# Layer-norm statistics by ScalarE's accumulated sums in a graph-network kernel

## The chip, the cores and the metric

The kernel runs on one core of a Trainium2 chip. The metric is the device time of one execution in microseconds (us). All times here come from repeated executions of the kernel before and from one execution that the hardware profiler recorded.

## The reference, cut to what matters

Four graph layers run one after the other on 4096 nodes with 256 features. Each adds its input to its result and normalises. The change touches the end of the second layer, where a norm with gain and offset is followed at once by the residual norm, and the top-p cut of the attention in that layer.

```python
def _layernorm(x, axis=-1, eps=1e-5):
    m = jnp.mean(x, axis=axis, keepdims=True)
    v = jnp.var(x, axis=axis, keepdims=True)
    return (x - m) / jnp.sqrt(v + eps)

def _top_p_attention(X, W1, W2, W3):
    q = X @ W1.T @ W2.T
    k = X @ W3.T
    probs = jax.nn.softmax(q @ k.T / TAU, axis=-1)
    idx = jnp.argsort(-probs, axis=-1)
    sp = jnp.take_along_axis(probs, idx, axis=-1)
    cs = jnp.cumsum(sp, axis=-1)
    keep_sorted = cs - sp < TOP_P
    ...
    return A / jnp.maximum(A.sum(-1, keepdims=True), 1e-12)

# _L1_gnn_ref: R is the normalised adjacency plus identity
for n in range(STEPS):          # STEPS = 2
    A = _top_p_attention(Xa, W1, W2, W3)
    Xf = R @ Xf
    Xa = A @ Xa
    Z = Z + Xf @ U1[n].T + Xa @ U2[n].T
h = X + Z
mu = h.mean(-1, keepdims=True)
var = jnp.mean((h - mu) ** 2, axis=-1, keepdims=True)
return (h - mu) / jnp.sqrt(var + LN_EPS) * ln_g + ln_b

# reference
x = _layernorm(x + _L0_gnn_ref(x, adj, L0_gnn_W), axis=-1)
x = _layernorm(x + _L1_gnn_ref(x, adj, ...), axis=-1)
x = _layernorm(x + _L2_gnn_ref(x, adj, L2_gnn_H_v), axis=-1)
x = _layernorm(x + _L3_gnn_ref(x, adj, adj, L3_gnn_weight, L3_gnn_bias), axis=-1)
```

## The kernel before

The nodes are cut into 32 blocks of 128 rows. The first three blocks of the adjacency are treated as dense, and the others through lists of their non-zero columns, whose rows GpSimd (POOL) gathers with indirect DMAs. The first 450 us compute layer 0, the next 550 us the first attention step. Then comes the loop that the change touches: the second attention step, one row block after the other, in `for I in range(NT + 1)` with NT = 32. A round I of that loop works on several blocks at once:

- block I+3: TensorE computes its logits (L630), and ScalarE (ACT) their exponentials (L701, and L704 with half the scale) in the first slots of the round;
- block I+2 and I+3: ACT evaluates sums of a threshold guess over the whole row (`sums`: L740 with Relu, L746 with Sign), and POOL moves the threshold by a chain of some twelve tiny operations (`secant`, L754 and L757);
- block I+1: VectorE (DVE) keeps the values over the threshold and sorts them (`keep_few`: L821, the MAX8 of L827, sorts in L804 and L806, the boundary value u), and then cuts the row at u with its ties counted (`cut`: L857 to L869, then L872 and the MATCH_REPLACE8 of L873);
- block I: TensorE turns the cut row in eight groups (L224), ACT copies each to SBUF (`eT`, L226), and TensorE multiplies (`psa`, L235); this is `weighted_sum`, which hands out a slot of other work in each group. The product with R for the same block runs in those slots (`r_ahead`, L1057 and L1062, gathers at L371);
- block I-1: `out_1`, the end of the layer: the two norms and the store. It is a generator in pieces. L1009 takes the product out of PSUM, `norm_scale` gives the statistics, L1013 applies the first norm on ACT, POOL applies gain, offset and residual (L1014 to L1016), `norm_scale` runs again, L1021 applies the second norm on ACT, L1023 on DVE computes the score of the next layer, and x2 is stored.

The whole loop stands under a schedule written by hand: for TensorE, ACT, DVE and POOL, instructions run in the order of the calls. SyncE's DMA queue is not part of it. Each `steps(gen)` runs a generator to its next `yield`; that is how the pieces are placed. `end` is the generator of `out_1`. In a round it is moved on at these places:

```python
            steps(few)
            steps(end)
            steps(few)
            ...
                    if g == 0:      # first slot of weighted_sum
                        run(second_sum)
                        run(first)
                        evals = at[I + 2]["sums"] if I + 2 < NT else none
                        steps(few)
                        steps(end)
                        steps(few)
```

The first of these, with the kernel before, is the first `norm_scale`, and the second is L1013 with POOL's three operations. `run(second_sum)` ends with L746, and `run(first)` is POOL's secant. The other places are in the printed function below, after `run(slot)`: `steps(end)`, then `steps(guessed)`, `run(guessed)`, `steps(end)`, and after `steps(cuts)` a `run(end)`, which runs what is left.

`ud` (L845) is u times -1.2 * 2^-24, computed on POOL, and the instruction at L865 makes from it the four thresholds of the cut: u itself, or a value just under u where ties are kept. `down8` holds 0 to -7 for the drop of surplus ties (L872). If the guarded test at the end (`failed`) finds a row that the fast path can't hold, a branch over all columns runs as well.

Of the kernel before, what the change touches and what calls it, by code (L numbers as in the profile page):

```python
# [11 lines left out]
F32 = mybir.dt.float32  # L12
BF16 = mybir.dt.bfloat16
I32 = mybir.dt.int32
AF = mybir.ActivationFunctionType
OP = mybir.AluOpType
AX = mybir.AxisListType

P = 128
N = 4096  # L20
D = 256
DA = 64
NT = N // P
EPS = 1e-5
# [28 lines left out]
FETCH = 3  # L53
LEAD, SPREAD = (5, 12), 0.75
NM = 4
GUESS = (1.2, -0.129)
SLOPE, AIM, NEAR, MOVE, FEW = 0.07, 16, 32, 1.5, 70
EXP_BITS = float(2 ** 23 / np.log(2))
# [16 lines left out]
def gnn_kernel(ctx: ExitStack, tc: tile.TileContext, x, pair, panels, W0, W1, W2T, W3T, U1T, U2T,  # L75
               ln_g, ln_b, Hv, W3L, b3, hubs, out):
    nc = tc.nc
    PSUM = bass.MemoryType.PSUM
    const = ctx.enter_context(tc.tile_pool(name="const", bufs=1))
# [44 lines left out]
    def one(name, dtype=F32, bufs=2):  # L124
        return small.tile([P, 1], dtype, name=name, tag=name, bufs=bufs)
# [40 lines left out]
        return t  # L166

    iota8 = iota([8], "iota8", [[1, 8]])
    down8 = const.tile([P, 8], F32, name="down8")
    nc.vector.tensor_scalar_mul(down8, iota8, -1.0)  # L170
    row = const.tile([P, 1], I32, name="row")
    nc.gpsimd.iota(row, [[1, 1]], base=0, channel_multiplier=1)

# [635 lines left out]
    def keep_few(a):  # L809


        I, e, s = a["I"], a["e"], a["s"]
        f = facts[1]["f"][:, I:I + 1]
        cand = pools["w2"].tile([P, NS, 8], F32, name="cand", bufs=1)
        ex = pools["w2"].tile([P, TOP], F32, name="ex", bufs=1)
        h = a["h"]
        low = small.tile([P, 2], F32, name="low")
        for c in range(2):
            w = tmp_tile([P, N // 2])
            ec = e[:, c * (N // 2):(c + 1) * (N // 2)]  # L820
            nc.vector.scalar_tensor_tensor(w, ec, h, ec, op0=OP.is_lt, op1=OP.mult, accum_out=low[:, c:c + 1])  # L821
            nc.gpsimd.tensor_scalar(f, low[:, c:c + 1], -1.0, f if c else s, op0=OP.mult, op1=OP.add)
            if c:
                nc.gpsimd.tensor_copy(ex[:, 0:1], f)
            yield
            for g in range(NS // 2):
                nc.vector.max(cand[:, c * (NS // 2) + g, :], w[:, g * SEG:(g + 1) * SEG])  # L827
            yield
        tgt = a["tgt"]
        nc.vector.tensor_reduce(facts[1]["h"][:, I:I + 1], cand[:, :, 7], AX.X, OP.max)  # L830
        top = pools["w2"].tile([P, TOP], F32, name="top", bufs=1)
        rest = pools["w2"].tile([P, NS * 8], F32, name="rest", bufs=1)
        sort_top(top, cand.rearrange("p a b -> p (a b)"), rest, TOP)
        nc.vector.tensor_tensor_scan(ex[:, 1:], ones.to_broadcast([P, TOP - 1]), top[:, :TOP - 1], f, op0=OP.mult, op1=OP.add)
        nc.gpsimd.tensor_copy(facts[1]["x"][:, I:I + 1], ex[:, TOP - 1:])
        kv = pools["w2"].tile([P, TOP], F32, name="kv", bufs=1)
        k = one("ks")
        nc.vector.scalar_tensor_tensor(kv, ex, tgt, top, op0=OP.is_lt, op1=OP.mult, accum_out=k)
        u, r = facts[1]["u"][:, I:I + 1], facts[1]["r"][:, I:I + 1]
        nc.vector.scalar_tensor_tensor(top, ex, tgt, top, op0=OP.is_ge, op1=OP.mult)  # L840
        nc.vector.tensor_reduce(u, top, AX.X, OP.max)
        nc.vector.tensor_scalar(kv, kv, u, 0.0, op0=OP.is_equal, op1=OP.add, accum_out=r)
        nc.vector.tensor_add(k, k, f)
        ud = a["ud"] = one("ud")
        nc.gpsimd.tensor_scalar(ud, u, -1.2 * 2.0 ** -24, None, op0=OP.mult)  # L845
        a["kr"], a["rk"] = one("kr", bufs=3), one("rk", bufs=3)
        nc.gpsimd.tensor_scalar(a["kr"], k, rinv[:, I:I + 1], None, op0=OP.mult)
        nc.vector.reciprocal(a["rk"], k)
        a["cand"], a["rest"] = cand, rest

    def cut(a):


        n, I, e, cand, rest = 1, a["I"], a["e"], a["cand"], a["rest"]
        u, r = facts[n]["u"][:, I:I + 1], facts[n]["r"][:, I:I + 1]
        ties = small.tile([P, NM], F32, name="ties")
        nc.vector.tensor_scalar(rest, cand.rearrange("p a b -> p (a b)"), u, None, op0=OP.is_equal)  # L857
        nc.vector.tensor_reduce(ties, rest.rearrange("p (a b) -> p a b", a=NM), AX.X, OP.add)
        left = small.tile([P, NM], F32, name="left")
        nc.vector.tensor_tensor_scan(left, ones.to_broadcast([P, NM]), ties, r, op0=OP.mult, op1=OP.subtract)  # L860
        nc.vector.tensor_add(ties, ties, left)
        nc.vector.tensor_scalar(ties, ties, 0.0, None, op0=OP.is_gt)
        d = facts[n]["d"][:, I:I + 1]
        nc.vector.scalar_tensor_tensor(left, left, 0.0, ties, op0=OP.min, op1=OP.mult, accum_out=d)
        nc.vector.tensor_scalar(ties, ties, a["ud"], u, op0=OP.mult, op1=OP.add)  # L865
        m = N // NM
        for g in range(NM):
            eg = e[:, g * m:(g + 1) * m]
            nc.vector.scalar_tensor_tensor(eg, eg, ties[:, g:g + 1], eg, op0=OP.is_gt, op1=OP.mult)  # L869
        yield  # L870
        drop = small.tile([P, 8], F32, name="drop")
        nc.vector.tensor_scalar(drop, down8, d, u, op0=OP.is_gt, op1=OP.mult)  # L872
        nc.vector.match_replace(e[:, ::-1], drop, e[:, ::-1], 0.0)  # L873

    def failed():
# [4 lines left out]
        for n in range(2):  # L880
            s, f, u, h, x, r = (facts[n][k] for k in "sfuhxr")
            nc.vector.tensor_tensor(c, h, u, op=OP.is_lt if n else OP.is_le)
            nc.vector.tensor_mul(ok, ok, c)
            if n:
                nc.vector.tensor_scalar(c, s, TOP_P, None, op0=OP.mult)
                nc.vector.tensor_tensor(x, x, c, op=OP.is_ge)
                nc.vector.tensor_mul(ok, ok, x)
                nc.vector.tensor_tensor(f, f, c, op=OP.is_lt)
                nc.vector.tensor_mul(ok, ok, f)
                nc.vector.scalar_tensor_tensor(ok, facts[n]["d"], -8.0, ok, op0=OP.is_ge, op1=OP.mult)  # L890
            else:
                nc.vector.scalar_tensor_tensor(ok, u, 0.0, ok, op0=OP.is_gt, op1=OP.mult)
                nc.vector.scalar_tensor_tensor(c, r, 1 - 2.0 ** -14, u, op0=OP.mult, op1=OP.is_gt)
                nc.vector.tensor_mul(ok, ok, c)
                nc.vector.scalar_tensor_tensor(ok, listed[:, :, 1], float(NB * P), ok, op0=OP.is_le, op1=OP.mult)
            nc.vector.scalar_tensor_tensor(ok, s, 1e-25, ok, op0=OP.is_gt, op1=OP.mult)
            nc.vector.scalar_tensor_tensor(ok, s, 1e35, ok, op0=OP.is_lt, op1=OP.mult)
# [81 lines left out]

    scores = const.tile([P, NT], F32, name="scores")  # L980

    def to_shift(m, rs):
        t = one("shift")
        nc.gpsimd.tensor_scalar(t, m, rs, -1.0, op0=OP.mult, op1=OP.mult)
        return t

    def scaled_rest(a, psr):

        xf = work.tile([P, D], F32, name="xf2", tag="nb")
        nc.scalar.activation(xf, psr[:, :D], AF.Copy, scale=a["kr"])  # L990
        return xf

    def norm_scale(st_of):
        st = small.tile([P, nc.vector.BN_STATS_DIM], F32, name="st")
        nc.vector.bn_stats(st, st_of)
        mv = small.tile([P, nc.vector.BN_AGGR_DIM], F32, name="mv")
        nc.vector.bn_aggr(mv, st)
        ve, rs = one("ve"), one("rs")
        nc.gpsimd.tensor_scalar(ve, mv[:, 1:2], EPS, None, op0=OP.add)
        nc.gpsimd.tensor_tensor(rs, ve, neg_half, OP.pow)  # L1000
        return rs, to_shift(mv[:, 0:1], rs)

    def out_1(a, psa):

        I = a["I"]
        x0 = pools["late"].tile([P, D], F32, name="x0")
        nc.sync.dma_start(x0, tab[rows(I), :D])
        h = work.tile([P, D], F32, name="y")
        nc.scalar.activation(h, psa[:, :D], AF.Copy, scale=a["rk"])  # L1009
        yield  # L1010
        rs, shift = norm_scale(h)
        yield
        nc.scalar.activation(h, h, AF.Identity, scale=rs, bias=shift)  # L1013
        nc.gpsimd.tensor_add(x0, x0, bb)  # L1014
        nc.gpsimd.tensor_mul(h, h, gb)
        nc.gpsimd.tensor_add(h, h, x0)  # L1016
        yield
        rs, shift = norm_scale(h)
        yield
        x2 = pools["late"].tile([P, D + 2], F32, name="x2", tag="o")  # L1020
        nc.scalar.activation(x2[:, :D], h, AF.Identity, scale=rs, bias=shift)  # L1021
        yield
        nc.vector.scalar_tensor_tensor(h, x2[:, :D], 1.0, hvb, op0=OP.mult, op1=OP.mult, accum_out=x2[:, D + 1:])  # L1023
        nc.gpsimd.memset(x2[:, D:D + 1], 1.0)
        nc.gpsimd.tensor_copy(scores[:, I:I + 1], x2[:, D + 1:])
        nc.sync.dma_start(x2d[rows(I), :], x2)
# [792 lines left out]
```

## Time and profile before

| | us |
|---|---|
| median of 11 runs | 2536.13 |
| lowest and highest run | 2533.56 and 2542.25 |
| the profiled execution, its own time | 2528.12 |
| its span, first to last instruction | 2526.3 |

Busy time in that span: PE (TensorE's matmuls) 2117.9, its weight loads (PEld) 1520.1, DVE 2087.4, POOL 1612.5, ACT 1477.2.

The span begins with the first instruction and ends with the last. Times in the views are us from the start of the span. A line such as L1013 is a line of the kernel before. The letter x with a number counts instructions; a bracket names the idle time ahead of an instruction and the engine and line that ended it. The page's rows of digits cut the span into 40 equal slices of 63 us, and each digit is the busy share in tenths. An instruction that gives a sum is followed by a readout (ACTIVATION_READ_ACCUMULATOR or DVE_READ_ACCUMULATOR) on the same engine.

The instructions that the change removes or touches, from the trace (median of one, in ns): bn_stats at L995 421 (x64), bn_aggr at L997 182 (x64), `ve` at L999 236, the power at L1000 568, `shift` at L984 264, `ud` at L845 240 (x32), L1009 475 (x32), L1013 608 (x32), L1021 619 (x32), POOL's L1015 727 (x32).

### The profile page before, as it was taken

Reading aid. Unit: us, or ns where it says so; the run is one execution under the profiler, and the core shown is the slowest. Engines: PE = TensorE matmul, PEld = TensorE weight load, DVE = VectorE, ACT = ScalarE, POOL = GpSimd, SP = SyncE. Lnnn points to the kernel's source line nnn. Section 1 sums busy time; section 2 is a strip of 40 time slices with the busy share of each in tenths; the row PEclk is TensorE's granted clock in tenths of the full one; section 3 lists DMA queues with packets and bytes.
Section 4 is the critical chain, followed back from the end, with each engine's and each line's share of the span. In section 5 each row is a group of like instructions: output and inputs, shape, how many; then the busy total and the mean of one; then the engine's idle time right before and its main releaser. Section 6 shows DMA issues by size and latency. Waiting matters only on the chain.

```text
span 2526.3 us, 37676 instructions
## 1 busy us (share of the span) xinstructions
PE 2117.9 (84%) x10692; PEld 1520.1 (60%) x10692; DVE 2087.4 (83%) x6433; ACT 1477.2 (58%) x2455; POOL 1612.5 (64%) x2648
## 2 busy tenths in 40 slices
PE   7888988799988887698888788888888877788995
PEld 5666666356555555576665566656656666556774
DVE  4788876799999983665899899999999996688588
ACT  0111111488888885565888889999999972434100
POOL 3343433366666665434888888888888883766375
PEclk8999999799999999899899999999999998899998
DMA  9887875456555556455111111111111123888795
GB/s 304 290 273 243 300 228 167 119 169 169 146 145 138 152 140 180 153 159 158 58 44 51 49 46 43 45 45 45 45 44 45 44 59 92 273 277 272 219 300 161
DMA packets 252842, 371.90 MB, mean 147 GB/s; under 512 B 40176, under 2 KB 161536, under 8 KB 252624
## 3 DMA queue, kind: packets, MB, share of 16 engines
q1 hardware_dynamic: 162528, 212.27, 26.3%
q0 software_dynamic: 41936, 120.07, 17.5%
q10 hardware_dynamic: 48160, 37.05, 4.4%
q8 instruction: 88, 1.44, 0.2%
q14 instruction: 130, 1.06, 0.1%
HBM read 314.23 MB, written 55.02 MB: 146 GB/s over the span
## 4 chain that ended last, share of the span: by engine, by line
DVE 30%; PE 14%; ACT 5%; POOL 4%; issue 4%; DMA 3%; DVEq 0%; SPq 0%; ACTq 0%; POOLq 0%
DVE cand L827 5%; DVE e L873 4%; PE acc L1620 4%; PE psa L235 4%; DVE tmp L821 4%; DVE e L869 3%; PE acc L1057 2%; DVE top L804 2%; DVE rest L806 2%; ACT junk L740 2%; POOL xg L371 1%; PE pt L224 1%; DVE vt L267 1%; PE lg L630 1%; DMA t3d<-t 1%
## 5 line engine op out<-in xcount | busy, mean ns | idle before, releaser
L235 PE MATMUL psa<-v,eT 128*128 128x256 f32 x2048 | 506.1, 394 | 74.3 <-ACT eT L226 74.0
L235 PEld LDWEIGHTS psa<-v,eT 128*128 128x128 f32 x2048 | 395.5, 197 | 150.3 <-ACT eT L226 96.1
L516 PE MATMUL acc<-xw,panel 128*128 128x257 f32 x1024 | 253.4, 395 | 16.9 <-DMA xw<-in_x 16.9
L740 ACT ACTIVATE junk<-e,h 128x4096 bf16<-128x4096 f32 x64 | 237.4, 3710 | 38.9 <-POOL h L720 28.3
L224 PE MATMUL pt<-ident,e 128*128 128x128 f32 x1024 | 158.9, 286 | 107.7 <-DVE e L873 64.1
L516 PEld LDWEIGHTS acc<-xw,panel 128*128 128x128 f32 x1024 | 194.1, 196 | 61.6 <-issue 30.3
L746 ACT ACTIVATE junk<-e,h 128x4096 bf16<-128x4096 f32 x62 | 230.8, 3722 | 0.1
L224 PEld LDWEIGHTS pt<-ident,e 128*128 128x128 f32 x1024 | 131.1, 148 | 151.9 <-issue 108.8
L827 DVE MAX8 cand<-tmp 128x8 f32<-128x128 f32 x1024 | 203.8, 276 | 1.1
L226 ACT COPY eT<-pt 128x512 f32<-128x512 f32 x256 | 144.9, 588 | 95.2 <-PE pt L224 94.5
L371 POOL DMA_INDIRECT pc<-in_pair,idx_a x130 | 127.9, 984 | 96.1 <-PE lists_ps L331 37.8
L1118 DVE MAX8 cand<-e 128x8 f32<-128x256 f32 x512 | 176.3, 411 | 3.7 <-ACT e L1110 3.7
L1148 ACT ACTIVATE marks<-e,mid 128x1024 bf16<-128x1024 f32 x128 | 140.2, 1143 | 50.6 <-DVE mid L1144 46.4
L371 POOL DMA_INDIRECT xg<-x2d,idx_x x130 | 131.6, 1012 | 54.8 <-issue 23.8
L371 POOL DMA_INDIRECT xg<-ttab,idx_x x130 | 128.6, 989 | 53.6 <-issue 24.1
L371 POOL DMA_INDIRECT xg<-qtab,idx_x x130 | 123.5, 950 | 59.2 <-issue 28.9
L869 DVE SCALAR_TENSOR_TENSOR e<-e,ties 128x1024 f32<-128x1024 f32 x128 | 156.0, 1281 | 2.9
L701 ACT ACTIVATE e<-lg 128x1024 f32<-128x1024 f32 x120 | 123.2, 1027 | 51.3 <-PE lg L630 51.3
L821 DVE SCALAR_TENSOR_TENSOR tmp<-e,h 128x2048 f32<-128x2048 f32 x64 | 150.7, 2355 | 2.3
L1107 PE MATMUL lg<-kT,qi 64*128 64x512 f32 x512 | 145.3, 643 | 3.3 <-DVE want L356 2.8
L630 PE MATMUL lg<-kT,qi 64*128 64x512 f32 x480 | 136.0, 643 | 14.3 <-ACT junk L704 14.0
L371 POOL DMA_INDIRECT xg<-y3d,idx_x x111 | 106.5, 960 | 64.6 <-PE acc L1620 42.1
(345 smaller groups left out, 5361.2 us busy)
## 6 DMA issues: line engine op xcount, KB each, us to landing
panel<-in_panels SPq DMA_DIRECT2D x200, 256.0 KB
e<-in_panels SPq DMA_DIRECT2D x64, 512.0 KB
pc<-pk SPq DMA_DIRECT2D x78, 256.0 KB
xg<-ttab SPq DMA_DIRECT2D x96, 128.0 KB
kT<-in_hubs SPq DMA_DIRECT2D x24, 512.0 KB
pc<-in_panels SPq DMA_DIRECT2D x32, 256.0 KB
tab<-xi ACTq DMA_DIRECT2D x33, 160.0 KB
pc<-pk SPq DMA_DIRECT2D x15, 320.0 KB
```

The lines of the kernel that those rows point to most:

```text
L224: nc.tensor.transpose(pt[:, k, :], e[:, (g * 4 + k) * P:][:, :P], ident)
L235: nc.tensor.matmul(ps[:, :D], eT[g][:, k, :], rhs[j][:, :D], start=(j == 0), stop=stop and j == NT - 1)
L371: nc.gpsimd.indirect_dma_start(out=o, out_offset=None, in_=src, in_offset=bass.IndirectOffsetOnAxis(ap=idx[:, c], axis=0))
L516: nc.tensor.matmul(ps[:, :D + 1], a[:, k, :], XW[j][:, :D + 1], start=(j == 0), stop=(j == NT - 1))
L630: nc.tensor.matmul(ps[:, h, :], qi[r, :], kT[r, (n * NC + c) * LC:][:, :LC], start=True, stop=True)
L740: nc.scalar.activation(junk_tile(), e, AF.Relu, bias=h, scale=-1.0, accum_out=part)
L746: nc.scalar.activation(junk_tile(), e, AF.Sign, bias=h, scale=-1.0, accum_out=below)
L821: nc.vector.scalar_tensor_tensor(w, ec, h, ec, op0=OP.is_lt, op1=OP.mult, accum_out=low[:, c:c + 1])
L827: nc.vector.max(cand[:, c * (NS // 2) + g, :], w[:, g * SEG:(g + 1) * SEG])
L869: nc.vector.scalar_tensor_tensor(eg, eg, ties[:, g:g + 1], eg, op0=OP.is_gt, op1=OP.mult)
L1107: nc.tensor.matmul(a["lg", c][:, k, :], a["qi"][r, :], kT[r, c * LC:(c + 1) * LC], start=True, stop=True)
L1118: nc.vector.max(a["cand"][:, b, :], a["e"][:, b * SEG0:(b + 1) * SEG0])
```

## The change

Both layer norms in `out_1` get their statistics from ACT instead of from DVE's bn_stats and bn_aggr. ACT's copy out of PSUM (L1009) also gives the sum of each row; POOL turns it into the negative mean; ACT squares the centred row and gives the sum of squares; POOL makes the scale and the shift. For the second norm, whose input POOL has just computed, ACT first copies the row for its sum. The output of the copy and of the squares goes to a bf16 tile, `aside`, which nobody reads. A `yield` between POOL's three operations and the second `norm_scale` is gone.

`ud` and POOL's operation for it are gone. The marks of kept ties carry the factor -2^-24 (`STEP`) and the thresholds are (marks + 1) times u; the count of surplus ties is scaled by the same factor, so `down8` becomes `up8` with the opposite test, and the guarded test compares with -8 STEP.

```diff
+STEP = -2.0 ** -24
-    down8 = const.tile([P, 8], F32, name="down8")
-    nc.vector.tensor_scalar_mul(down8, iota8, -1.0)
+    up8 = const.tile([P, 8], F32, name="up8")
+    nc.vector.tensor_scalar_mul(up8, iota8, -STEP)
 ...
-        ud = a["ud"] = one("ud")
-        nc.gpsimd.tensor_scalar(ud, u, -1.2 * 2.0 ** -24, None, op0=OP.mult)
 ...
-        nc.vector.tensor_scalar(ties, ties, 0.0, None, op0=OP.is_gt)
+        nc.vector.tensor_scalar(ties, ties, 0.0, STEP, op0=OP.is_gt, op1=OP.mult)
 ...
-        nc.vector.tensor_scalar(ties, ties, a["ud"], u, op0=OP.mult, op1=OP.add)
+        nc.vector.tensor_scalar(ties, ties, 1.0, u, op0=OP.add, op1=OP.mult)
 ...
-        nc.vector.tensor_scalar(drop, down8, d, u, op0=OP.is_gt, op1=OP.mult)
+        nc.vector.tensor_scalar(drop, up8, d, u, op0=OP.is_lt, op1=OP.mult)
 ...
-    def norm_scale(st_of):
-        st = small.tile([P, nc.vector.BN_STATS_DIM], F32, name="st")
-        nc.vector.bn_stats(st, st_of)
-        mv = small.tile([P, nc.vector.BN_AGGR_DIM], F32, name="mv")
-        nc.vector.bn_aggr(mv, st)
-        ve, rs = one("ve"), one("rs")
-        nc.gpsimd.tensor_scalar(ve, mv[:, 1:2], EPS, None, op0=OP.add)
-        nc.gpsimd.tensor_tensor(rs, ve, neg_half, OP.pow)
-        return rs, to_shift(mv[:, 0:1], rs)
+    def aside():
+        return small.tile([P, D], BF16, name="aside", bufs=1)
+
+    def norm_scale(total, y):
+
+        m, v, rs = one("m_y"), one("v_y"), one("rs")
+        nc.gpsimd.tensor_scalar(m, total, -1.0 / D, None, op0=OP.mult)
+        nc.scalar.activation(aside(), y, AF.Square, bias=m, accum_out=v)
+        nc.gpsimd.tensor_scalar(v, v, 1.0 / D, EPS, op0=OP.mult, op1=OP.add)
+        nc.gpsimd.tensor_tensor(rs, v, neg_half, OP.pow)
+        shift = one("shift")
+        nc.gpsimd.tensor_scalar(shift, m, rs, None, op0=OP.mult)
+        return rs, shift
 
     def out_1(a, psa):
 ...
-        nc.scalar.activation(h, psa[:, :D], AF.Copy, scale=a["rk"])
-        yield
-        rs, shift = norm_scale(h)
+        total = one("total")
+        nc.scalar.activation(h, psa[:, :D], AF.Copy, scale=a["rk"], accum_out=total)
+        yield
+        rs, shift = norm_scale(total, h)
         yield
         nc.scalar.activation(h, h, AF.Identity, scale=rs, bias=shift)
         nc.gpsimd.tensor_add(x0, x0, bb)
         nc.gpsimd.tensor_mul(h, h, gb)
         nc.gpsimd.tensor_add(h, h, x0)
-        yield
-        rs, shift = norm_scale(h)
+        total = one("total")
+        nc.scalar.activation(aside(), h, AF.Copy, accum_out=total)
+        rs, shift = norm_scale(total, h)
         yield
         x2 = pools["late"].tile([P, D + 2], F32, name="x2", tag="o")
         nc.scalar.activation(x2[:, :D], h, AF.Identity, scale=rs, bias=shift)
```

More of the change, by code (lines that the diff above doesn't have):

```diff
@@ L889, in failed @@
                 nc.vector.tensor_mul(ok, ok, f)
-                nc.vector.scalar_tensor_tensor(ok, facts[n]["d"], -8.0, ok, op0=OP.is_ge, op1=OP.mult)
+                nc.vector.scalar_tensor_tensor(ok, facts[n]["d"], -8.0 * STEP, ok, op0=OP.is_le, op1=OP.mult)
             else:
@@ L980, in gnn_kernel @@
     scores = const.tile([P, NT], F32, name="scores")
[L982 to L985, printed above, removed]
     def scaled_rest(a, psr):
```

## The prediction

> **What bounds the kernel now.** I read first the page's head and its 40 slices, to find the stage that the change touches:
>
> ```profile
> span 2526.3 us, 37676 instructions
> DVE  4788876799999983665899899999999996688588
> ACT  0111111488888885565888889999999972434100
> ```
>
> The two norms run in slices 18 to 34, where VectorE (DVE) and ScalarE (ACT) both show 8 and 9. Windows of 100 us inside it (columns: stretch, its length, then busy time of PE, PE's weight loads, DVE, ACT, POOL, the granted clock, the DMA share, GB/s):
>
> ```profile
> 1500.00:1600.00 100.00, 82.02 (x391) 60.54 (x389) 95.55 (x261) 91.24 (x113) 84.74 (x166) 0.98 0.14 43
> 1600.00:1700.00 100.00, 82.92 (x400) 61.06 (x400) 95.90 (x265) 91.72 (x112) 85.93 (x170) 1.00 0.14 42
> ```
>
> DVE is the bound (the missing 4% are hand-overs), but ACT and POOL are close behind. Next the order of one round of the loop over row blocks, engine by engine, in the timeline (start, length, instruction). ACT:
>
> ```profile
> 1566.60 1.06 ACT L226 COPY eT<-pt 128x512 f32<-128x512 f32 x2
> 1567.54 0.62 ACT L1021 ACTIVATE x<-y,shift,rs 128x256 f32<-128x256 f32 x1
> ...
> 1576.98 3.71 ACT L746 ACTIVATE junk<-e,h 128x4096 bf16<-128x4096 f32 x1
> ...
> 1580.68 0.59 ACT L1013 ACTIVATE y<-y,shift,rs 128x256 f32<-128x256 f32 x1
> 1581.17 0.57 ACT L226 COPY eT<-pt 128x512 f32<-128x512 f32 x1
> ```
>
> POOL:
>
> ```profile
> 1580.87 2.23 POOL L754 TENSOR_SCALAR below<-below 128x1 f32<-128x1 f32 x1 [0.84 <-ACT junk L746]
> ...
> 1587.04 0.30 POOL L754 TENSOR_SCALAR h<-h,b 128x1 int32<-128x1 int32 x1
> ...
> 1587.80 0.73 POOL L1014 TENSOR_TENSOR x<-x,bb 128x256 f32<-128x256 f32 x1
> 1588.48 0.73 POOL L1015 TENSOR_TENSOR y<-y,gb 128x256 f32<-128x256 f32 x1
> 1589.29 0.73 POOL L1016 TENSOR_TENSOR y<-y,x 128x256 f32<-128x256 f32 x1
> ```
>
> DVE:
>
> ```profile
> 1564.43 4.87 DVE L869 SCALAR_TENSOR_TENSOR e<-e,ties 128x1024 f32<-128x1024 f32 x4
> 1569.22 0.42 DVE L1023 SCALAR_TENSOR_TENSOR y<-x,hvb 128x256 f32<-128x256 f32 x1
> ...
> 1569.96 4.41 DVE L873 MATCH_REPLACE8 e<-drop,e 128x4096 f32<-128x4096 f32 x1
> ...
> 1574.67 2.35 DVE L821 SCALAR_TENSOR_TENSOR tmp<-e,h 128x2048 f32<-128x2048 f32 x1
> ```
>
> What to see: each engine runs exactly in the order in which the code calls it. After L1013 ACT goes on at once with an eT copy, which TensorE needs, while POOL finishes the sum h (L1016) only at 1590.02. First L995 of a round: 1561.46, next round 1593.62, so this round takes 32.16. Rounds are counted by the loop variable I. From the end of L746's readout in round 3 (1209.64) to that in round 29 (2059.84) there are 26 rounds in 850.2 us, 32.7 each.
>
> **Work moved.** Off DVE: bn_stats and bn_aggr, twice a round. Start to start they occupy 0.54 (1561.46 to 1562.00) and 0.56 (1576.94 to 1577.50): 1.10 per round, so DVE's own work is 32.16 - 1.10 = 31.06. Onto ACT: a readout at L1009 (0.19 long, the next instruction starts 0.09 after it), two Squares (nearest row L1013, 0.61, plus readout: at most 0.75) and a Copy with its sum (nearest row L936, 0.51, plus readout: 0.6). That is about 1.9 per round in occupancy. ACT's waits in this round (0.52, 0.65, 0.27, 0.75, 0.66, 0.48, all on TensorE) sum to 3.33, so ACT works 28.8 and would work 30.7. On POOL each norm goes from three tiny operations to four (+0.25 each, priced by L999's 0.24), less `ud` (0.24). By work alone nothing passes DVE's 31.06. [...]
>
> **Ties and up8.** The new constants leave the number of DVE instructions as it is; STEP takes `ud`'s place. DVE waited 28.4 us in all for `ud`, 16.2 of it in round 2, nothing in the steady rounds. What that frees in rounds 2 to 10 goes into the new waits below.
>
> **Three new waits**, from the code's order. (1) The Copy that sums h stands right behind L1013 on ACT and needs L1016. Behind it on ACT wait the second Square, the eT copies of this block, the exponentials of a later one, L740 and L746, and on them TensorE. (2) The first Square needs POOL's m, which POOL queues behind L822, which needs DVE's L821; behind the Square are eT copies and L746. (3) One yield is gone, so each later piece of `out_1` runs one call of `steps(end)` sooner. L1021 keeps its place on ACT (nothing lies between). L1023, which needs it, moves on DVE from behind L869 to ahead of L857, so the whole cut waits for ACT.
>
> **One round walked through**, t = 0 at the end of L746's readout.
> POOL's secant needs that readout: hand-over 0.09, `below` 0.19 (its smallest duration), the following operations to the end of h 4.14 (1583.20 to 1587.34), from L822 to the end of L1016 2.69. L1016 ends at 7.2. In the trace `below` took 2.23, ending at 1583.10 just after DVE's L821 (1583.04); if that recurs, 9.2. [...] In the new order DVE is in its MAX8 by then, and beside MAX8 the rows from 1583.20 on ran at their usual lengths, so I take 7.2 and keep 9.2 for the range.
> ACT: Copy 0.6, POOL's m with hand-overs 0.45, Square 0.75: t = 9.0. Then three slots, each an eT copy and two exponentials, 2.47 (1581.17 to 1583.64): 7.4. TensorE has run ahead, so its waits there vanish. From L740 to the end of L1021 9.8 (1558.36 to 1568.16): t = 26.2.
> DVE: hand-over 0.1, L1023 0.42, the cut from L857 to the end of L869 7.18 (1562.04 to 1569.22), from the drop to the end of L821's readout 7.46 (1569.56 to 1577.02): t = 41.4. (POOL's second secant starts at 24.7, takes 4.7, and its seven last operations end by about 36 even if L869 holds them: not late. ACT is through L740, two exponentials and L1009 at about 33: not late.)
> POOL: L822 and m with hand-overs 0.8. ACT: Square 0.7, two eT copies 0.95, L746 with readout 3.8: the next round's zero is at **47.6**.
> Cross-check on DVE: work 31.06; its last sort ends 16.2 after L821 (t = 10.0) and it then stands until 26.3, so 31.06 + 16.2 = 47.3. DVE goes from bound to waiter, and the ring ACT, DVE, POOL, ACT sets the time.
>
> **Sum.** 26 rounds: 26 x 47.6 - 850.2 = +387. Rounds 1 and 2 have TensorE's dense blocks (32 terms spread over 8 slots), which hide most of the stall. In round 1 L1023 already waited for L1021 until 1149.56; the cut and the rest behind it put the next L746 off by about 13. In round 2 TensorE reaches the product that needs the delayed eT copy at 1169.27, ACT gives it at about 1170.5; there +4. Round 29 lacks the exponentials: +9; rounds 30 and 31 have no secant: +4; the tail after the last L1009 gains a Copy and two round trips: +2. Total 387 + 17 + 15 = +419. The profiled execution took 2528.1 (span 2526.3 plus 1.8); with the change 2947. The median of the runs is 2536.1, 8 more, so **2955**.
>
> **Rivals.** *Faster:* the waits are covered, DVE stays the bound, each round falls to 31.06, and some of the 28.4 for `ud` comes back: 30 x 1.1 to that plus 28, 2475 to 2503. For it: DVE at 96%. Against it: ACT has 3.3 of slack, and the work takes 1.9 of that, so any stall over 1.4 decides; the order says 6.7 (from L1013's end at 0.5 to 7.2). *Only ACT's waits count:* if L1023 does not hold the cut, DVE has finished it by 24 and after L1023 needs 7.46: 34.2, then 6.2: a round of 40.4. That is 26 x 7.7 + 20 = +220: 2756. Against it: nothing in the code puts L1023 behind L857. *A longer ring:* the only ACT_TABLE_LOAD in the trace takes 1.28 us; if Square needed its own table, four switches a round are 5.1, all on the ring, +133: 3088. Against it: Copy, Sign, Relu, Identity and Exp share one load now. Or SP's queue puts x2d's store, which waits for POOL's L1024 at about 36, ahead of the next qi load; then the exponentials end near 41 and the ring is hardly longer. *It does not do what it says:* if the new thresholds did not cut where the old ones do, the kernel's guarded branch over all columns would run too, beyond any range here; but 1 - 2^-24 times u still rounds to the next number below u.
>
> **How the numbers follow.** Forecast ring 0.79; only ACT's waits 0.08; longer ring 0.09; faster 0.03; the branch 0.01. A ring of 44, if hand-overs and the four nearest-row prices are all too high and TensorE's head start does more, gives 2536 + 26 x 11.3 + 31 = 2861; a held secant, 49.6, gives 3007. I reach a little to both neighbours: 2830 to 3050. About 5 us (0.2%) is what a measurement can tell from no change. Faster 0.03, same 0.01, slower 0.96.
>
> **What would show it.** Right: L1023 idles some 16 us a round on ACT's L1021; the Copy idles about 6.7 on POOL's h; the first Square idles some 9 on m; DVE near 65% busy in the loop, POOL's gathers unchanged, stages before 1110 and after 2150 the same length. Wrong: eT copies that start right after L1013, a cut ahead of L1023, a second table load, or a round under 44 or over 50.

## The result, and the profile after

The changed kernel takes 3064.1 us (median of 8 runs, 3058.8 to 3071.1), the kernel before 2537.0 (31 runs): 1.207 times as long, 95% interval 1.206 to 1.2087. The direction was forecast, the mechanism too, but 3064 lies 14 us over the stated range and 109 over the forecast. The profiled execution took 3064.2 us, its span 3062.4.

The page's head and slices, as shown of before:

```profile
span 3062.4 us, 37734 instructions
DVE  5788867999995553746464646465656565568778
ACT  0111116888876655565656565665656565244300
PEclk8999998999999888777777777777777777889998
```

In the loop neither DVE nor ACT shows an 8 any more: no engine is the bound by its work, each one waits in turn. The granted clock, 0.97 over the loop before (1205 to 2050), is at 7 tenths (0.77 from 1200 to 2550). A window of the steady part, to set beside those of before:

```profile
1900.00:2000.00 100.00, 63.28 (x252) 45.20 (x252) 57.34 (x161) 60.50 (x83) 45.04 (x107) 0.77 0.10 28
```

DVE fell from 96 to 57, ACT from 92 to 60. One round in the timeline. The new lines are one off the old ones: L747 was L746, L1012 was L1013, L1015 was L1016, L868 was L869, L872 was L873, L822 was L821, and so are L227, L631, L702, L705, L716, L741 and L755; L994 is the Square, L1017 the Copy for the sum, L1021 and L1023 are as before. ACT:

```profile
1906.88 0.51 ACT L994 ACTIVATE aside<-y,m_y 128x256 bf16<-128x256 f32 x1 [8.37 <-POOL m_y L993]
...
1912.03 0.59 ACT L1012 ACTIVATE y<-y,shift,rs 128x256 f32<-128x256 f32 x1
1919.34 0.42 ACT L1017 ACTIVATE aside<-y 128x256 bf16<-128x256 f32 x1 [6.72 <-POOL y L1015]
...
1925.46 1.02 ACT L702 ACTIVATE e<-lg 128x1024 f32<-128x1024 f32 x1 [1.70 <-PE lg L631]
...
1929.76 0.58 ACT L227 COPY eT<-pt 128x512 f32<-128x512 f32 x1 [2.18 <-PE pt L225]
1930.83 1.02 ACT L702 ACTIVATE e<-lg 128x1024 f32<-128x1024 f32 x1 [0.48 <-PE lg L631]
```

POOL and DVE of the same round:

```profile
1912.21 0.19 POOL L755 TENSOR_SCALAR below<-below 128x1 f32<-128x1 f32 x1 [3.40 <-ACT junk L747]
...
1918.59 0.72 POOL L1015 TENSOR_TENSOR y<-y,x 128x256 f32<-128x256 f32 x1
```

```profile
1909.56 2.35 DVE L822 SCALAR_TENSOR_TENSOR tmp<-e,h 128x2048 f32<-128x2048 f32 x1
...
1932.98 0.16 DVE L716 TENSOR_REDUCE both_sums<-sq 128x2 f32<-128x8 f32 x1 [10.42 <-ACT junk L705]
1942.81 0.42 DVE L1023 SCALAR_TENSOR_TENSOR y<-x,hvb 128x256 f32<-128x256 f32 x1 [9.67 <-ACT x L1021]
...
1945.22 4.89 DVE L868 SCALAR_TENSOR_TENSOR e<-e,ties 128x1024 f32<-128x1024 f32 x4
...
1950.43 4.41 DVE L872 MATCH_REPLACE8 e<-drop,e 128x4096 f32<-128x4096 f32 x1
```

All three forecast waits stand in these lines, released by whom the prediction named: the first Square waits 8.37 for m (forecast 9), the Copy 6.72 for POOL's sum (6.7), L1023 9.67 for L1021, now with the whole cut behind it. The forecast had some 16 for this last wait. DVE stands 20 in two pieces: another 10.4 come just before, at `both_sums` (L716), which waits for the exponentials. What the prediction did not have are ACT's three waits in brackets from 1925 on.

**Where the 536 us of the two spans went.** The end of the MATCH_REPLACE8 over a whole row marks a round. Rounds 3 to 28 (26 of them) took 851.1 us before and 1332.7 after, 32.7 and 51.3 each: +481.5 (forecast +387). The rounds ahead of them +27 (forecast +17), those behind +16 (forecast +13), the tail and the stage behind it +5. The first cut ends 6 us later, in work that the change hardly touches; between executions this mark moves that much (1071.0 to 1081.7 in kernels that share that code).

### The profile page after: what moved, and what is told of

Same layout as the page of the kernel before. It is cut to its first block, busy times and chain, and to the rows that moved or that the text cites. A ratio compares the mean times of both kernels' runs of the same rounds, so it can differ in the third digit from the quotient of the medians.

```text
span 3062.4 us, 37734 instructions
## 1 busy us (share of the span) xinstructions
PE 2269.2 (74%) x10692; PEld 1613.9 (53%) x10692; DVE 2060.2 (67%) x6305; ACT 1528.0 (50%) x2679; POOL 1515.5 (49%) x2680
## 4 chain that ended last, share of the span: by engine, by line
DVE 19%; ACT 19%; PE 15%; POOL 8%; issue 4%; DMA 1%; DVEq 0%; ACTq 0%; SPq 0%; POOLq 0%
ACT junk L747 6%; DVE e L868 5%; DVE e L872 4%; PE psa L236 4%; ACT junk L741 4%; PE acc L1620 4%; PE lg L631 3%; DVE tmp L822 2%; ACT eT L227 2%; ACT e L702 2%; PE acc L1057 2%; ACT junk L705 2%; ACT aside L994 1%; POOL b L755 1%; PE po L443 1%
## 5 line engine op out<-in xcount | busy, mean ns | idle before, releaser
L236 PE MATMUL psa<-v,eT 128*128 128x256 f32 x2048 | 577.7, 435 | 117.4 <-ACT eT L227 117.4
L236 PEld LDWEIGHTS psa<-v,eT 128*128 128x128 f32 x2048 | 444.0, 222 | 226.6 <-ACT eT L227 152.2
L225 PE MATMUL pt<-ident,e 128*128 128x128 f32 x1024 | 177.8, 311 | 259.0 <-DVE h L789 229.3
L631 PE MATMUL lg<-kT,qi 64*128 64x512 f32 x480 | 162.1, 757 | 205.3 <-ACT junk L705 205.3
L225 PEld LDWEIGHTS pt<-ident,e 128*128 128x128 f32 x1024 | 149.0, 164 | 306.4 <-issue 264.0
L741 ACT ACTIVATE junk<-e,h 128x4096 bf16<-128x4096 f32 x64 | 237.5, 3711 | 28.2 <-POOL h L721 20.0
L1023 DVE SCALAR_TENSOR_TENSOR y<-x,hvb 128x256 f32<-128x256 f32 x32 | 13.6, 426 | 330.8 <-ACT x L1021 330.8
L747 ACT ACTIVATE junk<-e,h 128x4096 bf16<-128x4096 f32 x62 | 230.3, 3714 | 0.1
L716 DVE TENSOR_REDUCE both_sums<-sq 128x2 f32<-128x8 f32 x32 | 5.1, 160 | 309.2 <-ACT junk L705 306.5
L227 ACT COPY eT<-pt 128x512 f32<-128x512 f32 x256 | 142.3, 579 | 112.2 <-PE pt L225 112.1
L702 ACT ACTIVATE e<-lg 128x1024 f32<-128x1024 f32 x120 | 122.7, 1022 | 89.5 <-PE lg L631 89.5
L755 POOL TENSOR_SCALAR below<-below 128x1 f32<-128x1 f32 x64 | 12.2, 190 | 310.9 <-ACT junk L747 305.7
L1148 ACT ACTIVATE marks<-e,mid 128x1024 bf16<-128x1024 f32 x128 | 140.2, 1143 | 49.6 <-DVE mid L1144 45.3
L631 PEld LDWEIGHTS lg<-kT,qi 64*128 64x128 f32 x480 | 41.9, 214 | 233.1 <-ACT junk L705 212.6
L1057 PE MATMUL acc<-xg,pc 128*128 128x256 f32 x452 | 162.2, 474 | 0.2 <-DMA xg<-ttab 0.2
```

Of the source, the lines that this page charges most:

```text
L225: nc.tensor.transpose(pt[:, k, :], e[:, (g * 4 + k) * P:][:, :P], ident)
L227: nc.scalar.copy(eT[g], pt)
L236: nc.tensor.matmul(ps[:, :D], eT[g][:, k, :], rhs[j][:, :D], start=(j == 0), stop=stop and j == NT - 1)
L631: nc.tensor.matmul(ps[:, h, :], qi[r, :], kT[r, (n * NC + c) * LC:][:, :LC], start=True, stop=True)
L702: nc.scalar.activation(both(e, c), ps, AF.Exp, accum_out=s8[:, c:c + 1])
L741: nc.scalar.activation(junk_tile(), e, AF.Relu, bias=h, scale=-1.0, accum_out=part)
```

## The experiments

The experiments ran on four chips, on each of them beside the kernel before. On three of the chips the kernel before took 2864 to 2885 us instead of 2537. The difference lies outside the loop: in e4, on one of them, the first cut ends at 1346 us and in the profile before at 1071, the stretch behind the last cut is 57 us longer, while the steady rounds agree (31.9 and 32.0). Why it is so was not looked into. So what follows is compared by the ratio to the kernel before on the same chip, and by the mean round, from the end of round 2 to the end of round 28 (the fourth and the thirtieth MATCH_REPLACE8 over a whole row; 32.7 before, 51.3 changed). A steady round is one of the later ones.

### e1: the yield put back

```diff
         nc.gpsimd.tensor_add(h, h, x0)
+        yield
         total = one("total")
```

> The changed kernel with the removed yield put back between POOL's three operations and the Copy that sums h, so that the Copy, the second Square and L1023 stand where the second norm and L1023 stood before. Theory (a ring of three waits, most of it from where the Copy and L1023 stand): ACT goes from L1013 straight to the eT copy, L1023 is behind the cut again, and what stays is the first Square's wait for m and 1.3 more of ACT's work behind the last eT copy: a round of about 37 us where the changed kernel has 51.3, in all about 2655 us (2600 to 2720). Rival (the statistics themselves are too dear on ACT and POOL, wherever they stand): the work is the same, so the time stays above 2950.

Measured: ratio 1.0616 (1.0576 to 1.0656), round 39.2. With the same work on every engine, two thirds of the loss are gone: they were the price of the place, not of the work. The round is 2 us longer than expected. In the timeline ACT and DVE still show:

```profile
2030.97 0.51 ACT L994 ACTIVATE aside<-y,m_y 128x256 bf16<-128x256 f32 x1 [3.42 <-POOL m_y L993]
...
2061.07 0.42 DVE L1024 SCALAR_TENSOR_TENSOR y<-x,hvb 128x256 f32<-128x256 f32 x1 [5.70 <-ACT x L1022]
```

The first Square's wait is there as forecast; the wait for x2 is longer than in my walk, since the second norm now does its Copy, Square and two trips to POOL between the last eT copy and L1022.

### e2: L1023 behind the cut again

```diff
         nc.scalar.activation(x2[:, :D], h, AF.Identity, scale=rs, bias=shift)
         yield
+        yield
         nc.vector.scalar_tensor_tensor(h, x2[:, :D], 1.0, hvb, ...
```

> The changed kernel with one empty yield ahead of L1023, which puts L1023 on DVE back behind the first part of the cut and leaves the Copy behind L1013. Theory: the first part of the cut (6.95 us) goes into DVE's idle time, the Copy's stall stays: a round of about 44.4 us, in all about 2880 us (2840 to 2920). Rival (the Copy's stall is hidden and L1023's wait is the whole cost): the time falls to about 2600. Second rival (the Copy's stall is the whole cost): it stays at 3064.

Measured: ratio 1.1127 (1.1089 to 1.1166), 321 us more than the kernel before where 343 were expected; round 44.4, as expected. The round fell by 6.8, close to the 6.95 of the cut that went into DVE's idle time. Neither the Copy's wait nor L1023's is the whole.

### e3: two logits tiles

```diff
+    banks(tp=2, ms=1, lg=2)
     end = second_sum = none
 ...
+    banks(tp=2, ms=2)
     enter(late=2)
```

> The changed kernel with two PSUM tiles for the logits in the loop (and one instead of two for psa; accA is not used there). The three exponential slots took 12.3 us of a round instead of the 7.4 of my walk. Theory: TensorE could not run ahead since the next logits wait for the only logits tile; with two, the waits of 1.7, 2.2 and 0.5 nearly vanish, a round of about 47 us, in all about 2952 us (2930 to 2980). Rival (TensorE is slow after its idle time, at a granted clock of 0.76): the waits stay, 3030 to 3064.

Measured: ratio 1.1395 (1.1348 to 1.1441), 402 us over the kernel before (expected 415); round 47.1. This is the run that settles what the prediction missed. From the eT copy behind the second Square to L741, the three slots took on average 12.3 us in rounds 3 to 28 of the changed kernel and 8.2 here (7.6 to 8.0 in most rounds, 9.0 to 9.3 in the others); in the kernel before they took 10.0. In the changed kernel TensorE stood in ACT's stall before the logits of slot 2, and was slow when it went on:

```profile
1923.34 2.08 PE L631 MATMUL lg<-kT,qi 64*128 64x512 f32 x4 [7.41 <-ACT junk L705]
...
1929.65 1.13 PE L631 MATMUL lg<-kT,qi 64*128 64x512 f32 x4
```

With the second tile (PE, then ACT) the same logits are made inside the stall, and the exponentials of slot 2 wait for nothing (the round is one of those with 9.3):

```profile
2214.79 1.13 PE L631 MATMUL lg<-kT,qi 64*128 64x512 f32 x4
```

```profile
2224.21 1.05 ACT L702 ACTIVATE e<-lg 128x1024 f32<-128x1024 f32 x1
```

The rival is not empty: the slow clock is real (0.50 behind the stall of the changed kernel, last section), and in e3 the product behind the stall took 3.78 (at 2221.90, after 5.35 of idle time), the one at 2212.53 took 1.89. But without the wait for the tile the slots are 4.2 us shorter all the same.

### e4: the tie thresholds alone

The hunks of the change with STEP, up8 and without ud, applied to the kernel before; nothing of the norms.

> The kernel before with the second part of the change alone: thresholds by STEP and up8, no ud on POOL. Theory: DVE's 28.4 us of waits for ud go; of the 16.2 in round 2 only 1 to 2 count, since L1023 waits there for L1021 until 1197; some 12 are from rounds 3 to 10: about 2524 us (2512 to 2533). Rival (POOL's gathers, not ud, set those rounds through kr and the second secant): no change, 2537.

Measured: ratio 0.9954 (0.993 to 0.9978), 14.3 us less in the medians (2864.3 to 2850.1; expected 13 less). By itself this part of the change helps by half a per cent.

### e5, e6, e11: each wait by itself, in the kernel before

```diff
# e5
         nc.gpsimd.tensor_add(h, h, x0)
+        nc.scalar.activation(small.tile([P, D], BF16, name="aside", bufs=1), h, AF.Copy)
         yield
# e6
             run(guessed)
-            steps(end)
+            steps(end, 2)
# e11: norm_scale_act is norm_scale of the change
-        nc.scalar.activation(h, psa[:, :D], AF.Copy, scale=a["rk"])
+        total = one("total")
+        nc.scalar.activation(h, psa[:, :D], AF.Copy, scale=a["rk"], accum_out=total)
         yield
-        rs, shift = norm_scale(h)
+        rs, shift = norm_scale_act(total, h)
```

> The kernel before with one added instruction a round: a Copy of h to a tile that nobody reads, on ACT right behind L1013's place, after POOL's three operations in the code. All statistics stay on DVE. It is the first of the three waits by itself. Theory: ACT stands until POOL has summed h, 7 to 9 us after L746, and the round becomes the ring eT, L746, POOL's secant and sum, Copy, three slots of 12.3, 9.8 to the end of L1021, L1023, L873: 41.6 to 43.6 us instead of 32.0, in all about 255 us over the kernel before (ratio near 1.10). Rival (the cost is in the statistics, a Copy of 0.4 us is lost in ACT's slack): no change.

> The kernel before with L1023 called one place sooner, so that on DVE it stands ahead of the cut; nothing else. It is the third wait by itself. Theory: DVE waits for L1021 with the whole cut behind it: a round of about 38.5 us instead of 32.0, some 165 us over the kernel before (ratio near 1.065). Rival (L1021 comes early enough when ACT does not stall): within 1% of the kernel before.

> The kernel before with the statistics of the first norm alone by ACT's sums, as in the changed kernel; the second norm stays with bn_stats on DVE, L1023 behind the cut. It is the second wait by itself. Theory: the eT copies come some 2.4 us later behind L873, of which about 1 is slack: a round of 33.4 to 34.1 us instead of 32.0, ratio near 1.018 (1.01 to 1.03). Rival (the Square's wait on m is long but off the ring): no change or, by the 0.54 us that DVE saves, a round of 31.5.

Measured: the Copy alone 1.1146 (1.1119 to 1.1173), round 43.1. L1023 alone 1.0733 (1.0707 to 1.0758), round 39.2. The first Square alone 1.0254 (1.0203 to 1.0304), round 35.5, steady 35.0. The waits of the first two (in 18 rounds of the trace each):

```profile
ACT aside L1017 <- POOL y L1016: 154.1, 18, 8.9
```

```profile
DVE y L1023 <- ACT x L1021: 126.5, 18, 7.7
```

A single instruction of 0.4 us costs 10.4 us a round by its place. Over the kernel before the three are +10.4, +6.5 and +2.8 a round, 19.7 together, and the changed kernel has +18.5: they lie one behind the other on one ring and nearly add up. The first Square alone is 1 to 2 dearer than expected, and its wait for m is only part of its price: in e11's trace it waits 1.5 us a round (26.1 in 17 rounds), and L1023 waits 2.5 for L1021 (44.4 in 18). How the 2.8 come about was not followed further.

### e7: m ahead of L822's step

```diff
-            steps(few)
             steps(end)
             steps(few)
+            steps(few)
```

> The changed kernel with the first norm's statistics called ahead of the step of keep_few with L822, so that POOL's m does not stand behind the operation that needs L822. It takes the second wait away. Theory: the eT copy then waits for the transposes behind L872 alone, 2.4 us sooner: a round of 48.8 us instead of 51.3, 60 to 65 us under the changed kernel. Rival (the first Square's wait of 8 us on m is itself the cost): a round of 43 us.

Measured: 1.2064 (1.2035 to 1.2094), round 51.1: no gain, and neither theory's number. The Square's wait fell (3.02 at 1741.54, 8.37 in the changed kernel), but with L747 ending sooner POOL's `below` now meets the second L822, as it had in the kernel before (POOL, then DVE):

```profile
1699.10 1.82 POOL L755 TENSOR_SCALAR below<-below 128x1 f32<-128x1 f32 x1 [3.47 <-ACT junk L747]
```

```profile
1698.52 2.35 DVE L822 SCALAR_TENSOR_TENSOR tmp<-e,h 128x2048 f32<-128x2048 f32 x1
```

`below` takes 1.82 instead of 0.19 and ends with L822 (1700.92 and 1700.87). L747 starts 2.1 us sooner behind L872 than in the changed kernel (2.6 instead of 4.7); `below` gives back 1.6 of it, and the three slots, 12.7 instead of 12.3, the rest. What holds `below` beside L822 the traces do not show.

### e8, e9, e10: the statistics on ACT, placed by hand

Beside the hunks shown, `norm_scale` is also split behind m, a `yield` stands ahead of the Copy and behind each m, and the old calls of `steps(end)` in the first slot and behind `run(guessed)` are gone.

```diff
# e8, calls of steps(end): m ahead of L822's step, first Square behind run(second_sum),
# L1012 and POOL's sum at the end of slot 1, Copy in slot 3, second Square in slot 4
+                        steps(end)          # behind run(second_sum)
+                    if g == 1:
+                        steps(end)
                     if g in (3, 4):
+                        steps(end)
                         steps(evals)
 ...
-            run(end)
+            last = end
             end = out_1(at.pop(I), psa) if I < NT else none
             steps(end)
             run(cuts)
+            run(last)
# e9: in slot 3 steps(end, 2), none in slot 4
# e10: e9 with the two banks(...) lines of e3
```

> All statistics on ACT as in the changed kernel, each step called where its input is long there: m ahead of L822's step, the first Square behind L747, L1012 and POOL's sum at the end of slot 1, the Copy in slot 3, the second Square in slot 4, L1023 behind the second part of the cut. ACT, POOL and DVE do the same work as in the changed kernel. Theory (only the places cost): DVE is the bound again without its 1.1 us of statistics, a round of 31.1 to 32.3 us, ratio to the kernel before 0.985 to 1.0. Rival (the statistics are too dear on ACT): a round over 36, ratio over 1.04.

Measured: 1.0518 (1.0491 to 1.0545), round 38.1, steady 37 to 38. Not what the theory said, and the rival's number. The timelines name the reason (POOL, then DVE): the second v waits for the Square in slot 4, POOL's four gathers and the second secant queue behind it, and DVE waits for the secant. It was still a place.

```profile
1721.44 1.22 POOL L999 TENSOR_SCALAR v_y<-v_y 128x1 f32<-128x1 f32 x1 [4.80 <-ACT aside L998]
```

```profile
1735.86 0.16 DVE L789 TENSOR_TENSOR h<-h,b 128x1 int32<-128x1 int32 x1 [6.99 <-POOL b L755]
```

> The kernel with the statistics placed by hand, and the second Square called one slot sooner, right behind the Copy in slot 3. There POOL's v waited for that Square from 1716 to 1721 us with four gathers, L719, L721 and the second secant queued behind it, and DVE's L789 waited 7 us for the secant. Theory (the place of the Square is the rest of the cost): the secant starts at L747's end and is no longer late. Then ACT is next: 30.7 us of work and about 2.7 of waits for TensorE, a round of about 33.4 us instead of 37.5, ratio to the kernel before near 1.015 (1.005 to 1.03). Rival (something else than the Square holds POOL): a round over 36.

> The same with two PSUM tiles for the logits and one for psa in the loop, so that ACT's waits for logits go as well. Theory: ACT needs about 31.5 us a round, DVE 31.1, a round of 31.4 to 32.3 us, ratio to the kernel before 0.98 to 1.0. Rival (the waits for logits turn into waits for the transposes, since TensorE is the bound in slots 1 to 3): a round as without the second tile.

Measured: e9 1.0093 (1.0062 to 1.0123), round 34.4, steady between 32 and 35.5; e10 1.0011 (0.998 to 1.0042), round 33.4, steady 32.1. A window of e10:

```profile
1900.00:2000.00 100.00, 84.44 (x386) 62.01 (x387) 93.72 (x247) 95.11 (x133) 71.76 (x176) 0.95 0.15 43
```

ACT is busy as DVE was before (95), DVE 94. So in the steady rounds the statistics as such, where nobody waits for them, cost little and gain nothing: what DVE is spared, ACT hasn't got to spare. But e10 has the new thresholds too, which alone give 0.5% (e4); beside e4 it is 0.6% slower. Its steady round is 32.1 to e4's 31.9, and its rounds 3 and 4 are longer (44.3 and 37.2 to 34.2 and 34.2); why was not looked into. Nor does a run have the second logits tile with all statistics left on DVE, so what the tile is worth by itself is open.

### e12: the second norm alone on ACT

e10's places for the second norm and its two logits tiles, bn_stats for the first norm, with e4's thresholds.

> The kernel before with the tie thresholds of the change, two PSUM tiles for the logits, and the statistics of the second norm alone on ACT, Copy and Square both in slot 3; the first norm keeps bn_stats on DVE, L1023 stands behind the second part of the cut. Theory: ACT saves the first Square (0.6 us) against the version with both norms, and DVE still saves 0.56: ACT 31.4, DVE 31.5, a round of 31.5 to 32.0 us, ratio to the kernel before 0.988 to 0.997, so level with or just under the version with the thresholds alone. Rival (POOL's gathers, now behind the Square in slot 3, make the second secant late): a round over 32.3, ratio 1.0 or more.

Measured: 0.9948 (0.9926 to 0.997), steady round 32.0, as expected: level with e4, which has the thresholds alone and nothing moved. Of the versions tried, these two beat both kernels; e4 does it with fewer edits.

## Why the prediction was wrong, point by point

*What bounds, and the order.* Right: DVE had the most work, and the order of the calls on each engine decided who waits. *Work moved.* Right in the main: e10, with the same work as the changed kernel, is level with the kernel before, and 0.6% behind e4. The Square took 0.51 and the Copy 0.42, under the nearest rows of 0.61 and 0.51. *Ties.* By themselves they give 14 us (e4); in the profiles rounds 1 and 2 are 4 us shorter and rounds 3 to 28 together 7. The sum took nothing for them, since the new waits were to swallow it; no run tests that.

*The three waits.* All three are there, and each move costs by itself (e5, e6, e11). Taking away the third gives 6.8 a round (e2), the first and the third together 12.1 (e1). Taking away the second gives nothing (e7), since `below` is then held.

*The walk through one round.* By the trace from 1912.13 on, forecast and measured:

| term | forecast | measured |
|---|---|---|
| L746/L747's end to POOL's sum | 7.2 | 7.2 |
| Copy, m, Square | 1.8 | 1.4 |
| **three slots of eT copy and exponentials** | **7.4** | **12.3** |
| L740/L741 to the end of L1021 | 9.8 | 9.8 |
| L1023 and the cut | 7.7 | 7.3 |
| drop to the end of L821/L822 | 7.5 | 7.4 |
| to the next L746/L747's end | 6.2 | 5.8 |
| round | 47.6 | 51.2 |

The step that failed is the sentence "TensorE has run ahead, so its waits there vanish". The 7.4 was three times the first slot of the round shown; all three slots of that same round took 9.9, from 1581.17 to the L740 behind them at 1591.05. The step cost 4.9 a round; the other terms were 1.3 too dear together, which by luck hid a part of it. 3.6 x 26 is 94 us, nearly the whole of the 109. TensorE had run ahead by the transposes of one slot, and then its next logits waited until ACT had read the last ones: in this loop `banks(tp=2, ms=2)` leaves the logits a single tile, while the stage before has two (`banks(lg=2)`). e3 gives the logits a second tile: the slots fall to 8.2 and the round to 47.1.

The clock made that wait dearer: it was granted at 0.50 from 1923 to 1927, and at 1.00 beside the same chain of the kernel before (1583 to 1588). From the logits at 1923.34 to the transposes at 1929.12 the chain took 5.78. The same chain in the profile before:

```profile
1583.82 1.13 PE L630 MATMUL lg<-kT,qi 64*128 64x512 f32 x4 [0.21 <-ACT junk L704]
...
1587.14 0.60 PE L224 MATMUL pt<-ident,e 128*128 128x128 f32 x4
```

It took 3.32: an estimate of 2.5 of the 4.9 is the clock, and the rest are waits that the kernel before has as well (its 9.9 to the 7.4).

The 7.2 to POOL's sum came out for the reason given, but by little: the second L822 ended at 1911.9 and `below` began at 1912.21, beside the MAX8, and took 0.19. In e7 they met.

*The range.* Its upper end was a held secant, 49.6 or 3007, and a little more, 3050. The unknown that it did not bound was TensorE's head start: with the waits of the round shown (0.75, 0.66, 0.48; 26 x 1.9 is 49 us) on top of that upper end, the range would have held the result, though the secant was not held. *The rivals.* None came. The time is near the 3088 of the longer ring, but by a cause that this rival did not name: the trace has one table load, of 1.28 us, as before. A round over 50 was among the prediction's own signs of being wrong.

## What to carry to other kernels

Before moving an operation to an engine with slack, write down what stands behind it in that engine's order of calls and how late its input is at that very place: 0.4 us of work cost 10 us a round (e5). When an engine that feeds others is stalled, don't assume that its neighbours use the time to run ahead; count the buffers between them. And a yield or call that moves later pieces by one place changes the order on every engine that those pieces use.

## What the hardware showed that was not expected

TensorE's clock in the stall. Windows of the changed kernel (granted clock is the third number from the end) right after the wait of 7.4 us, and from 4 us later on:

```profile
1923.00:1925.00 2.00, 1.66 (x4) 0.51 (x4) 0.00 (x0) 0.76 (x3) 1.58 (x2) 0.50 0.23 66
...
1927.00:1929.00 2.00, 2.00 (x7) 1.59 (x7) 0.00 (x0) 0.58 (x2) 0.85 (x3) 0.64 0.39 100
1929.00:1931.00 2.00, 2.00 (x11) 1.00 (x10) 0.00 (x0) 0.76 (x2) 0.00 (x0) 1.00 0.04 12
```

The clock is 0.50 and in the end 1.00, and the same four logits products take 2.08 and 1.13 us. 0.50 stands there after 7.4 us of idle time, 0.64 from 1927 to 1929, and 1.00 from 1929 on, nearly 6 us after TensorE went on. What sets these times was not looked into. The stall comes in 26 rounds one after the other (1256 to 2538): after 6.8 to 7.6 us of idle time the four products take 2.08 each time, at a granted clock of 0.50 in the 2 us from their start, and 6.5 us after their start the clock is 1.00. By the estimate of 2.5 us above this is some 5% of a round.
